# The sums of the LSTM weights' quarters: made in every phase, or made once and loaded

## The chip, the cores and the metric

The kernel runs on one core of a Trainium2 chip. The metric is the device time of one execution in microseconds (us); a lower time is better. The chip offers TensorE (PE in the profile; its weight loads are PEld), VectorE (DVE), ScalarE (ACT), GpSimd (POOL) and SyncE (SP), which issues most DMAs. POOL can issue DMAs too.

## The reference, cut to what matters

The model has four layers on x of 128 graphs, 64 nodes and 256 features. Each normalises x, cuts it at zero, runs a graph network and adds the result to x. The change lies in layer 0, which is two graph convolutions followed by four LSTMs with windows of 1, 2, 3 and 4 nodes:

```python
h = relu(einsum('ts,bsh->bth', adj, x @ Wg0 + bg0))
h = relu(einsum('ts,bsh->bth', adj, h @ Wg1 + bg1))
for p in range(1, 5):
    nw = T // p
    wins = h[:, :nw * p, :].reshape(B * nw, p, H)
    last = lstm_last(Wih[p - 1], Whh[p - 1], bih[p - 1], bhh[p - 1], wins)
    h = h.at[:, arange(nw) * p + (p - 1), :].set(last)
```

and in the LSTM, from a zero state, for every step:

```python
g = x_t @ Wih.T + h @ Whh.T + bias
i, f, gg, o = split(g, 4)
c = sigmoid(f) * c + sigmoid(i) * tanh(gg)
h = sigmoid(o) * tanh(c)
```

Each of Wih and Whh is 1024 x 256 in float32 for each window.

## The kernel before

**Stages.** The 8192 tokens are 16 chunks of 512, or 4 groups of 2048. In the profiled execution the convolutions of all chunks take the first 190 us, the LSTM phases follow until about 1255 us, and layers 1 to 3 fill the rest. Half of the groups stay in the on-chip memory for the LSTM (hTs0); the output of the convolutions for the other half waits in DRAM (hmem).

**The convolutions.** `graph_convolutions(n)` is a generator for one chunk: it loads x three chunks ahead (`load_x`, L540, four buffers), normalises (statistics on DVE, L96; scaling on ACT, L120), aggregates, projects and aggregates again. A loop over 20 values of n moves the chunks under way on by one step each; the tables of later layers (`edge_tables`, `late_tables`) are made in small steps between them. One of these is dinv (L247) on POOL.

**The products of an LSTM.** A product of a weight and an operand is not made from its four quarters with eight smaller products, but with seven, from sums of quarters of the weight and sums of blocks of the operand. For each gate q, `product` issues these with the numbers 1 to 7. On the side of the weight the factors are: 1 is a11, 2 is a12, 3 is s4, 4 is a22, 5 is s1, 6 is s2 and 7 is a11 - a21, where s1 = a21 + a22, s2 = s1 - a11 and s4 = a12 - s2. The number 6 follows the pair 1 and 2, then 7, 5, 3 and 4 (`gate`, L780). The operand's sums are `xop`, made in `prepare` (L700): by ACT copies and DVE sums (L724 to L735), or on POOL when the step beside is a first one ("apart"). The sums of a state h are made on DVE (L858 to L862).

**The weights.** `Weights(kind, w)` (L494) loads one weight of 1024 KB from its input (L500) with one DMA on SP and makes the four sums for all gates on POOL (L512). Weights of the kind "ih" have two buffers, those of "hh" one. Windows 1 and 2 get theirs during the convolutions (n == 2, L652). There are eight phases: windows 1 to 4 for the first half of the groups, and again for the second. When a phase ends, `phase_over` orders the "ih" weight two phases on, eight slots later, and makes the "hh" weight of the next phase at once. So each weight of windows 1 to 4 that a phase uses is loaded and summed twice in a run; there is no "hh" for window 1. After the last phase the buffer of an "ih" weight serves as `x_first`, the first input of layer 1 (L1009).

**The order.** Instructions given to `late` keep the order in which the program makes them; the others are placed by a scheduler, which also places DMAs on SP's and POOL's queues. Each queue then runs in order: an instruction that waits holds up those behind it. A pool's tile of the same tag takes the place of an earlier one when that is released.

Of the kernel before, what the change touches and what calls it, by code (L numbers as in the profile page):

```python
# [9 lines left out]
F32 = mybir.dt.float32  # L10
# [4 lines left out]
ALU = mybir.AluOpType  # L15
AX = mybir.AxisListType

P = 128
T = 64
D = 256  # L20
# [3 lines left out]
MAX_SKIP = 4  # L24
# [7 lines left out]
def gnn_stack_kernel(ctx: ExitStack, tc: tile.TileContext, a: dict, out: bass.AP):  # L32
    nc = tc.nc
# [5 lines left out]
    dram = ctx.enter_context(tc.tile_pool(name="dram", bufs=1, space=bass.MemoryType.DRAM))  # L39
# [4 lines left out]
    def bank():  # L44
        return psums["now"].tile([P, 512], F32, tag="bank", name="bank", bufs=psums["banks"])
# [32 lines left out]
    def late(ins):  # L78

        tc.keep_in_program_order(ins)  # L80
# [4 lines left out]
    class Norm:  # L85


        def __init__(self, xt, root_on_scalar=False, keep=late, mv=None):
            self.xt, self.root_on_scalar, self.keep, self.h, self.mv = xt, root_on_scalar, keep, None, mv
            self.known = mv is not None  # L90
            if mv is None:
                self.st = stat.tile([P, 4, 6], F32, tag="ln_st", name="ln_st")
                self.mv = stat.tile([P, 4, 2], F32, tag="ln_mv", name="ln_mv")
# [79 lines left out]
    def transpose_features(h, dst, ip, keep=None):  # L173

        p = bank()
        for i2 in range(2):
            for c in range(2):
                k = (i2 * 2 + c) * P
                ins = nc.tensor.transpose(p[:, k : k + P], h[:, 2 * ip + i2, c * P : (c + 1) * P], ident)
                if keep and k == 0:  # L180
                    keep(ins)
        nc.scalar.activation(
            dst[:, :, ip * 256 : (ip + 1) * 256].rearrange("p c (i t) -> p i c t", i=2),
            p.rearrange("p (i c t) -> p i c t", i=2, c=2),
            AF.Relu,
        )
# [96 lines left out]
    keep = tabs.tile([P, E], F32, tag="keep", name="keep")  # L283
# [201 lines left out]
    with ExitStack() as l0:  # L485
        wsp = l0.enter_context(tc.tile_pool(name="wsp", bufs=1))
# [4 lines left out]

        class Weights:  # L494
            def __init__(self, kind, w, keep=lambda ins: None):
                bufs = 2 if kind == "ih" else 1
                t = wsp.tile([P, 2, 4, 2, P], F32, tag=f"w{kind}", name=f"w{kind}", bufs=bufs)
                s = wsp.tile([P, 3, 4, P], F32, tag=f"s{kind}", name=f"s{kind}", bufs=bufs)
                keep(
                    nc.sync.dma_start(  # L500
                        out=t.rearrange("p k q j m -> p k (q j m)"), in_=a[f"W{kind}T"][:, w - 1]
                    )
                )
                a11, a12, a21, a22 = t[:, 0, :, 0, :], t[:, 1, :, 0, :], t[:, 0, :, 1, :], t[:, 1, :, 1, :]
                s1, s2, s4 = s[:, 0], s[:, 1], s[:, 2]
                for o, x, y, op in (
                    (s1, a21, a22, ALU.add),
                    (s2, s1, a11, ALU.subtract),
                    (s4, a12, s2, ALU.subtract),
                    (a21, a11, a21, ALU.subtract),  # L510
                ):
                    keep(nc.gpsimd.tensor_tensor(o, x, y, op))  # L512
                self.of = {1: a11, 2: a12, 3: s4, 4: a22, 5: s1, 6: s2, 7: a21}

            def __call__(self, k, q):
                return self.of[k][:, q, :]

        bias = w0.tile([P, MAX_SKIP, 8], F32, tag="bias", name="bias")
        bias2 = w0.tile([P, MAX_SKIP, 8], F32, tag="bias2", name="bias2")
# [2 lines left out]
        weights = {}  # L522


        with ExitStack() as conv:
# [4 lines left out]
            def cpool(name, bufs):  # L530
                return conv.enter_context(tc.tile_pool(name=name, bufs=bufs, reuse_waits="tile"))
# [3 lines left out]
            wc = cpool("wc", 1)  # L535
# [34 lines left out]
            p = bank()  # L570
# [66 lines left out]

            tables = chain(edge_tables(), late_tables())
            under_way = []
            for n in range(NCH + 4):  # L640
                if n < NCH:
                    under_way.append(graph_convolutions(n))

                turns = under_way[-1:] + under_way[:-1] if n < NCH else list(under_way)
                if n == 1:
                    turns += under_way[-1:]
                for one in turns:
                    if next(one, 0) == 0:
                        under_way.remove(one)
                    if n >= 3:  # L650
                        next(tables, None)
                if n == 2:  # L652
                    weights["ih", 0], weights["ih", 1] = Weights("ih", 1), Weights("ih", 2)
                    weights["hh", 1] = Weights("hh", 2)
                    late(nc.vector.tensor_tensor(bias, bias, bias2, ALU.add))
            for _ in tables:
                pass
# [207 lines left out]
        steps, phases = [], []  # L865
        for half in range(2):
            ga, gb = 2 * half, 2 * half + 1
            for w in range(1, MAX_SKIP + 1):
                ph = len(phases)
# [82 lines left out]
        for slot in range(len(tasks) + 2):  # L952
            new = tasks[slot] if slot < len(tasks) else None
            if slot == len(tasks):

                for _ in norm_steps:
                    pass
                first_hT = gp.tile([P, 4 * NMAX], F32, tag="gate", name="hT1_first")
                first_hT = first_hT[:, : 2 * CHUNK].rearrange("p (c t) -> p c t", c=2)
                for ip in range(2):  # L960
                    transpose_features(norms1[0].h, first_hT, ip, late)
            if new:
                step = steps[new[0]]
                one = step.gate(new[1])
                next(one)
            if len(flight) > 1:
                old = flight.pop(0)
                next(old[1], None)
                if new:
                    some_out(slot)  # L970
                measure(2)
                next(flight[-1][1])
            elif flight and not new:
                old = flight.pop(0)
                next(old[1], None)
            else:
                old = None
                if flight:
                    next(flight[-1][1])
            if new:  # L980
                next(one)
                flight.append((new, one))
                at, k = new[0], new[2]
                some_out(slot)
            measure(2)
            if new:

                new_half = at + 1 < len(steps) and at and steps[at + 1].w == 1 < step.w
                if k == len(step.gates) - (1 if new_half else 2) and at + 1 < len(steps):
                    steps[at + 1].prepare(step)  # L990
                if step.w == MAX_SKIP and step.t == 2 and k < 2 and step.g < NGR - 1:
                    for u in range(2):
                        n = 4 * step.g + 2 * u + k
                        later.append((slot, "x", n))
            while later and later[0][0] <= slot:
                _, kind, n = later.pop(0)
                residual[n] = fetch_x(n)
            next(norm_steps, None)
            while later_weights and later_weights[0][0] <= slot:
                _, ph = later_weights.pop(0)  # L1000
                weights["ih", ph] = Weights("ih", phases[ph], late)
            if old:
                (at, q, k), step = old[0], steps[old[0][0]]
                if k == len(step.gates) - 1:
                    if at + 1 == len(steps) or steps[at + 1].phase != step.phase:
                        phase_over(step.phase)
                    if step.phase == len(phases) - 1 and step.t == 1 and step.g == NGR - 1:

                        t_ = wsp.tile([P, 2, 4, 2, P], F32, tag="wih", name="x_first", bufs=2)  # L1009
                        flat = t_.rearrange("p k q j m -> p k (q j m)")  # L1010
                        norms1 = {}
                        for n in range(2):
                            xt = flat[:, n, :].rearrange("p (i d) -> p i d", i=4)
                            nc.sync.dma_start(out=xt, in_=xa[n])
                            norms1[n] = Norm(xt)
                        norm_steps = first_norms1(norms1)
                    if step.w == MAX_SKIP and step.t == MAX_SKIP - 1:
                        outs += [(slot + 1, step.g, c, u, ip) for c in range(2) for u in range(2) for ip in range(2)]
# [6 lines left out]
    with ExitStack() as l1:  # L1025
# [32 lines left out]
        for g, c, u, ip in last_outs:  # L1058
            if not ip:
                n = 4 * g + 2 * u + c  # L1060
# [524 lines left out]
    with ExitStack() as l2:  # L1585
# [55 lines left out]
        with ExitStack() as dense2:  # L1641
# [67 lines left out]
            with ExitStack() as first_dense:  # L1709
# [43 lines left out]
                for slot, (pr, m2) in enumerate(tasks):  # L1753
                    n = slot + 3
# [131 lines left out]
        for k in range(2):  # L1886
            f = t4.tile([P, 4, P], F32, tag=f"field{k}", name=f"field{k}", bufs=1)
# [409 lines left out]
```

## Time and profile before

| | |
|---|---|
| median of 3 runs | 1953.12 us (1952.43 to 1953.27) |
| the profiled execution | 1953.8 us, span 1952.0 us |
| TensorE's granted clock | 0.998 |
| PE busy | 1914.7 us, 98% |
| POOL busy | 463.7 us, 24% |
| moved by DMA | 135.57 MB, mean 69 GB/s |

A line of a timeline gives the start in us from the span's start, the duration, the engine, the line of the kernel, the operation, the tile written and the tiles read, the shape and how many were merged; in brackets stands the idle time of the engine just before and what ended it. A matmul of 128x256 in float32 starts 0.22 us after the one before when nothing holds it up; its own duration in the timeline is longer, since matmuls overlap. In the lines of DMA issues the last number is the median time from issue to landing in us. In lines of waits stand who waited, for whom, the total in us, how often and the longest.

### The profile page before, as it was taken

What the parts mean: (1) busy time and instruction counts of PE and PEld (TensorE: products, weight loads), DVE (VectorE), ACT (ScalarE), POOL (GpSimd) and SP (SyncE); (2) the same over time, 40 slices, a digit from 0 to 9 for tenths busy, and PEclk for the clock granted to TensorE, in tenths of its full rate; (3) what the DMA queues carried; (4) which work ended last, traced back from release to release, by engine and by line L of the source; (5) the groups of instructions that cost most, each with busy time, mean ns of one, the idle gap of its engine ahead of it and who ended that gap; (6) DMA issues with size and microseconds to landing.
All of it is one profiled execution on the core that took longest, in us unless ns stands there. A gap on an engine that the chain in (4) does not pass through costs nothing. (4 is left out here: it accounts for less than half of the span.)

```text
span 1952.0 us, 25195 instructions
## 1 busy us (share of the span) xinstructions
PE 1914.7 (98%) x9150; PEld 1394.8 (71%) x9150; DVE 1329.1 (68%) x2506; ACT 1162.7 (60%) x2169; POOL 463.7 (24%) x614
## 2 busy tenths in 40 slices
PE   9999999999999999999999999999999999999998
PEld 7777468866678874788666788876666775544787
DVE  8775675574475567755744755788788777787887
ACT  4353775564565547755644656588786556592554
POOL 3000031140030002310400200166775510000584
PEclk9999999999999999999999999999999999999999
DMA  7513000010010044000100100342334841022112
GB/s 262 186 50 108 0 22 1 1 44 0 1 43 1 1 151 151 22 1 1 44 0 1 44 1 17 125 166 76 114 136 164 291 152 54 1 66 85 44 66 87
DMA packets 63885, 135.57 MB, mean 69 GB/s; under 512 B 6673, under 2 KB 41361, under 8 KB 61457
## 3 DMA queue, kind: packets, MB, share of 16 engines
q1 hardware_dynamic: 59824, 124.33, 18.7%
q0 software_dynamic: 3328, 9.44, 1.3%
q8 instruction: 72, 1.18, 0.2%
q14 instruction: 53, 0.43, 0.1%
q10 hardware_dynamic: 608, 0.20, 0.0%
HBM read 87.55 MB, written 46.40 MB: 69 GB/s over the span
## 5 line engine op out<-in xcount | busy, mean ns | idle before, releaser
L773 ACT ACTIVATE gate<-gate,bias 128x256 f32<-128x256 f32 (+2 forms) x368 | 247.1, 678 | 176.2 <-DVE gate L789 94.2
L745 PE MATMUL pa<-xop,sih 128*128 128x256 f32 (+2 forms) x1056 | 342.4, 417 | 4.9 <-DVE gate L799 4.7
L745 PEld LDWEIGHTS pa<-xop,sih 128*128 128x128 f32 x1056 | 198.4, 190 | 76.1 <-issue 18.9
L745 PE MATMUL pc<-xop,wih 128*128 128x256 f32 (+2 forms) x736 | 251.1, 423 | 0.0
L789 DVE TENSOR_TENSOR gate<-pb,gate 128x256 f32<-128x256 f32 (+2 forms) x184 | 87.5, 476 | 223.6 <-PE pb L745 151.3
L745 PE MATMUL pa<-lstm_h,shh 128*128 128x256 f32 (+1 forms) x672 | 212.7, 398 | 0.0
L745 PEld LDWEIGHTS pc<-xop,wih 128*128 128x128 f32 x736 | 139.8, 190 | 51.2 <-issue 22.5
L806 DVE TENSOR_TENSOR gate<-pc,gate 128x256 f32<-128x256 f32 (+2 forms) x184 | 87.5, 476 | 110.7 <-PE pc L745 110.1
L1149 ACT ACTIVATE lr<-pair 128x1024 f32<-128x1024 f32 x128 | 124.3, 1024 | 44.0 <-ACT xv L1133 16.2
L745 PEld LDWEIGHTS pa<-lstm_h,shh 128*128 128x128 f32 x672 | 127.7, 190 | 30.2
L745 PE MATMUL pc<-lstm_h,whh 128*128 128x256 f32 (+1 forms) x448 | 141.8, 398 | 0.0
L788 ACT COPY gate<-pa 128x256 f32<-128x256 f32 (+2 forms) x184 | 76.0, 413 | 85.6 <-PE pa L745 85.1
L1114 PE MATMUL bank<-wlv,hT 128*128 128x260 f32 x480 | 116.3, 383 | 4.4 <-DVE xq L1125 3.2
L799 DVE TENSOR_TENSOR gate<-pa,gate 128x256 f32<-128x256 f32 (+2 forms) x184 | 87.3, 475 | 41.4 <-PE pa L745 40.6
L773 ACT ACTIVATE gate<-pa,bias 128x256 f32<-128x256 f32 (+2 forms) x184 | 93.9, 510 | 31.1 <-PE pa L745 29.3
L793 ACT COPY gate<-pa 128x256 f32<-128x256 f32 (+2 forms) x184 | 75.3, 409 | 56.2 <-PE pa L745 55.1
L745 PE MATMUL pa<-xop,wih 128*128 128x256 f32 (+1 forms) x320 | 101.6, 399 | 1.4 <-ACT xop L724 1.2
L1114 PEld LDWEIGHTS bank<-wlv,hT 128*128 128x128 f32 x480 | 87.9, 190 | 20.5 <-DVE xq L1125 5.5
L745 PE MATMUL pb<-xop,wih 128*128 128x256 f32 (+1 forms) x320 | 100.6, 398 | 0.0
L745 PEld LDWEIGHTS pc<-lstm_h,whh 128*128 128x128 f32 x448 | 85.1, 190 | 20.1
L512 POOL TENSOR_TENSOR shh<-whh 128x512 f32<-128x512 f32 x6 | 7.6, 1270 | 379.9 <-DMA whh<-in_WhhT 257.1
L796 ACT COPY gate<-pc 128x256 f32<-128x256 f32 (+2 forms) x136 | 57.9, 425 | 53.0 <-PE pc L745 52.4
(380 smaller groups left out, 4024.5 us busy)
## 6 DMA issues: line engine op xcount, KB each, us to landing
field<-keep SPq DMA_DIRECT2D x4, 2304.0 KB, 13.0
wih<-in_WihT SPq DMA_DIRECT2D x8, 1024.0 KB, 7.0
xres<-in_x SPq DMA_DIRECT2D x16, 512.0 KB, 4.5
xa<-xres POOLq DMA_DIRECT2D x16, 512.0 KB, 3.8
xin<-xb SPq DMA_DIRECT2D x16, 512.0 KB, 3.8
h<-xb SPq DMA_DIRECT2D x16, 512.0 KB, 3.6
xin<-in_x SPq DMA_DIRECT2D x15, 512.0 KB, 6.2
out_x<-h SPq DMA_DIRECT2D x15, 512.0 KB, 2.9
```

The lines of the kernel that those rows point to most:

```text
L512: keep(nc.gpsimd.tensor_tensor(o, x, y, op))
L745: ins = nc.tensor.matmul(p[:, : self.N], weights[kind, self.phase](k, q), x[k], start=first_ and kind == "ih", stop=kind == "hh" or not se ...
L773: nc.scalar.activation(out, in_, AF.Tanh if q == 2 else AF.Sigmoid, bias=bias[:, self.w - 1, 2 * q + j : 2 * q + j + 1],)
L788: nc.scalar.copy(blk[0, 0], pa[:, :N])
L789: nc.vector.tensor_tensor(blk[0, 0], pb[:, :N], blk[0, 0], ALU.add)
L793: nc.scalar.copy(blk[1, 0], pa[:, :N])
L796: (nc.vector.tensor_copy if not self.t and self.w > 1 else nc.scalar.copy)(blk[1, 1], pc[:, :N])
L799: nc.vector.tensor_tensor(blk[1, 1], pa[:, :N], blk[1, 1], ALU.add)
L806: nc.vector.tensor_tensor(blk[1, 0], pc[:, :N], blk[1, 0], ALU.add)
L1114: ins = nc.tensor.matmul(o, hTs[n][:, k, i * P : (i + 1) * P], wlv[:, k, cols], start=k == 0, stop=k == 1)
L1149: nc.scalar.activation(lr, p, AF.Relu)
```

## The change

During the convolutions, the first use of a weight fills one tile of seven parts in the order of the products, [128, 7, 4, 128] (1792 KB): four DMAs bring a11, a12, a21 and a22 to the parts 0, 1, 6 and 3, and POOL makes the sums in place. POOL then stores the tile in DRAM (`quarters0`). The weights of windows 1 and 2 stay where they are for their first phase. The weights of windows 3 and 4 are made in halves of two gates, in eight rounds, in a tile `ahead` with one buffer, one round for each n from 4 on. Every later use is one load of 1792 KB from `quarters0` and has no sums.

```diff
+        quarters0 = {
+            (kind, w): dram.tile([P, 7, 4, P], F32, tag=f"q{kind}{w}", name=f"q{kind}{w}")
+            for kind in ("ih", "hh")
+            for w in range(1, MAX_SKIP + 1)
+        }
+
+        def quarter_weights(v, kind, w, q):
+
+            given = a[f"W{kind}T"][:, w - 1].rearrange("p k (q j m) -> p k q j m", q=4, j=2)
+            for at, k, j in ((0, 0, 0), (1, 1, 0), (6, 0, 1), (3, 1, 1)):
+                nc.sync.dma_start(out=v[:, at], in_=given[:, k, q, j, :])
+            a11, a12, s4, a22, s1, s2, a21 = (v[:, at] for at in range(7))
+            for o, x, y, op in (
+                (s1, a21, a22, ALU.add),
+                (s2, s1, a11, ALU.subtract),
+                (s4, a12, s2, ALU.subtract),
+                (a21, a11, a21, ALU.subtract),
+            ):
+                nc.gpsimd.tensor_tensor(o, x, y, op)
+            nc.gpsimd.dma_start(out=quarters0[kind, w][:, :, q, :], in_=v)
+
         class Weights:
-            def __init__(self, kind, w, keep=lambda ins: None):
-                bufs = 2 if kind == "ih" else 1
-                t = wsp.tile([P, 2, 4, 2, P], F32, tag=f"w{kind}", name=f"w{kind}", bufs=bufs)
-                s = wsp.tile([P, 3, 4, P], F32, tag=f"s{kind}", name=f"s{kind}", bufs=bufs)
-                keep(
-                    nc.sync.dma_start(
-                        out=t.rearrange("p k q j m -> p k (q j m)"), in_=a[f"W{kind}T"][:, w - 1]
-                    )
+            def __init__(self, kind, w, first_time=False, keep=lambda ins: None):
+                self.v = wsp.tile(
+                    [P, 7, 4, P], F32, tag=f"w{kind}", name=f"w{kind}", bufs=2 if kind == "ih" else 1
                 )
-                a11, a12, a21, a22 = t[:, 0, :, 0, :], t[:, 1, :, 0, :], t[:, 0, :, 1, :], t[:, 1, :, 1, :]
-                s1, s2, s4 = s[:, 0], s[:, 1], s[:, 2]
-                for o, x, y, op in (
...
-                    keep(nc.gpsimd.tensor_tensor(o, x, y, op))
-                self.of = {1: a11, 2: a12, 3: s4, 4: a22, 5: s1, 6: s2, 7: a21}
+                if first_time:
+                    quarter_weights(self.v, kind, w, slice(0, 4))
+                else:
+                    keep(nc.sync.dma_start(out=self.v, in_=quarters0[kind, w]))
 
             def __call__(self, k, q):
-                return self.of[k][:, q, :]
+                return self.v[:, k - 1, q, :]
...
+            ahead = [(kind, w, q) for w in (3, 4) for kind in ("ih", "hh") for q in (0, 2)]
             for n in range(NCH + 4):
...
+                if n > 3 and ahead:
+                    kind, w, q = ahead.pop(0)
+                    v = wc.tile([P, 7, 2, P], F32, tag="ahead", name="ahead")
+                    quarter_weights(v, kind, w, slice(q, q + 2))
                 if n == 2:
-                    weights["ih", 0], weights["ih", 1] = Weights("ih", 1), Weights("ih", 2)
-                    weights["hh", 1] = Weights("hh", 2)
+                    weights["ih", 0], weights["ih", 1] = Weights("ih", 1, True), Weights("ih", 2, True)
+                    weights["hh", 1] = Weights("hh", 2, True)
...
-                weights["ih", ph] = Weights("ih", phases[ph], late)
+                weights["ih", ph] = Weights("ih", phases[ph], keep=late)
...
-                        t_ = wsp.tile([P, 2, 4, 2, P], F32, tag="wih", name="x_first", bufs=2)
-                        flat = t_.rearrange("p k q j m -> p k (q j m)")
+                        t_ = wsp.tile([P, 7, 4, P], F32, tag="wih", name="x_first", bufs=2)
+                        flat = t_.rearrange("p s q m -> p (s q m)")[:, : 8 * D].rearrange("p (n x) -> p n x", n=2)
```

The on-chip memory for the weights stays the same in all (wih and sih, whh and shh were 8192 and 6144 bytes of a partition); `ahead` takes 7168 bytes of a partition during the convolutions. The products, their order and their operands are the same.

More of the change, by code (lines that the diff above doesn't have):

```diff
@@ L489, in gnn_stack_kernel @@
         hmem = {n: dram.tile([P, 2, CHUNK], F32, tag=f"hm{n}", name=f"hm{n}") for n in range(NCH // 2, NCH)}
-        class Weights:
-            def __init__(self, kind, w, keep=lambda ins: None):
-                bufs = 2 if kind == "ih" else 1
-                t = wsp.tile([P, 2, 4, 2, P], F32, tag=f"w{kind}", name=f"w{kind}", bufs=bufs)
-                s = wsp.tile([P, 3, 4, P], F32, tag=f"s{kind}", name=f"s{kind}", bufs=bufs)
-                keep(
-                    nc.sync.dma_start(
-                        out=t.rearrange("p k q j m -> p k (q j m)"), in_=a[f"W{kind}T"][:, w - 1]
-                    )
-                )
-                a11, a12, a21, a22 = t[:, 0, :, 0, :], t[:, 1, :, 0, :], t[:, 0, :, 1, :], t[:, 1, :, 1, :]
-                s1, s2, s4 = s[:, 0], s[:, 1], s[:, 2]
-                for o, x, y, op in (
[L507 to L512, printed above, removed]
-                self.of = {1: a11, 2: a12, 3: s4, 4: a22, 5: s1, 6: s2, 7: a21}
```

## The prediction

> **What bounds the kernel now.** I read the page first, then the busy time by stretches, then PE, POOL, DVE and DMA through the stretches where the weight sums run.
>
> ```profile
> PE 1914.7 (98%) x9150; PEld 1394.8 (71%) x9150; DVE 1329.1 (68%) x2506; ACT 1162.7 (60%) x2169; POOL 463.7 (24%) x614
> ...
> DMA  7513000010010044000100100342334841022112
> ```
>
> PE is busy for 98% of the span, so a change that leaves the matmuls alone can only move PE's few pauses. DMA digits (48.8 us each) are high in the first two: the convolutions start with much traffic and end with little.
>
> ```profile
> 0.00:190.00 190.00, 185.81 (x953) 140.70 (x953) 131.27 (x361) 78.47 (x148) 17.66 (x26) 1.00 0.45 153
> 262.00:405.00 143.00, 142.44 (x644) 121.84 (x643) 89.00 (x156) 88.37 (x184) 28.73 (x32) 1.00 0.05 15
> 405.00:555.00 150.00, 149.47 (x535) 101.10 (x534) 83.63 (x121) 80.38 (x143) 19.73 (x15) 1.00 0.04 13
> 555.00:712.00 157.00, 154.71 (x722) 134.60 (x721) 88.94 (x151) 85.92 (x178) 20.15 (x17) 1.00 0.06 22
> 40.00:60.00 20.00, 19.96 (x105) 15.36 (x106) 19.39 (x57) 9.25 (x19) 0.00 (x0) 1.00 1.06 356
> 80.00:100.00 20.00, 19.79 (x106) 14.52 (x105) 16.20 (x40) 6.78 (x13) 0.00 (x0) 1.00 0.09 27
> ```
>
> The columns are PE, PEld, DVE, ACT and POOL busy, PE's granted clock, DMA share and GB/s. In the convolutions (first row) PE pauses 4.2 us of 190; in the LSTM phases with windows of 2, 3 and 4 it pauses 0.6, 0.5 and 2.3 us. The clock is full. The gain is to come from the LSTM rows, and any loss from the first.
>
> **What the sums cost now.** The move out of window 3 into window 4:
>
> ```profile
> 556.77 1.27 POOL L512 TENSOR_TENSOR shh<-whh 128x512 f32<-128x512 f32 x1 [128.25 <-DMA whh<-in_WhhT]
> 558.12 1.33 POOL L512 TENSOR_TENSOR shh<-shh,whh 128x512 f32<-128x512 f32 x1
> ...
> 562.56 1.78 POOL L724 COPY xop<-hT 128x256 f32<-128x256 f32 x2 [0.46 <-ACT gate L773]
> ```
>
> Four sums take 5.3 us here. The operand copies (L724) behind them wait another 0.46 us for ACT, so POOL's order does not delay them. What the sums do is slow DVE. The same DVE instruction in the first half (under a sum) and in the second half (its sums start 0.36 us later, at 1090.40):
>
> ```profile
> 557.08 1.24 DVE L734 TENSOR_TENSOR xop<-xop 128x256 f32<-128x256 f32 x1
> ...
> 1090.04 0.42 DVE L734 TENSOR_TENSOR xop<-xop 128x256 f32<-128x256 f32 x1
> ```
>
> and PE at the same two places:
>
> ```profile
> 557.09 1.03 PE L745 MATMUL pb<-xop,wih 128*128 128x256 f32 x4
> 558.71 0.70 PE L745 MATMUL pa<-xop,sih 128*128 128x256 f32 x2 [0.60 <-DVE gate L799]
> ...
> 1090.04 1.03 PE L745 MATMUL pb<-xop,wih 128*128 128x256 f32 x4
> 1090.90 0.65 PE L745 MATMUL pa<-xop,sih 128*128 128x256 f32 x2
> ```
>
> From the four pb products to the next pa product is 1.62 us in the first half and 0.86 in the second: the sums cost PE 0.76 us there, and the trace holds its own control.
>
> **The change part by part.** *LSTM, removed:* 11 of the 14 sets of sums, 11 x (1.27 + 1.33 + 1.27 + 1.28) = 57 us of POOL. POOL is not the bound; what counts is three sorts of place.
> (a) 558.71: 0.76 us and 0.05 of a slower restart (0.70 against 0.65): 0.8. Bounds 0 to 0.8; the control says 0.8.
> (b) Window 2 into 3, at 408.24 and 941.22. L735 takes 1.24 us under a sum and 0.50 without, and PE then idles 0.46 us on DVE's L799, which ends at 408.18. 0.74 us sooner it would end at 407.44, but ACT's copy out of the same pa (L788) ends only at 407.96, so PE gains 0.2 to 0.3. Bounds 0 to 0.7 each; I take 0.25 twice, since ACT is the next in line: 0.5.
> (c) 569.95 and 1101.61, idle 1.06 and 0.49 us, also on DVE's L799. Here the slow DVE steps (L858 at 1.80 against 1.22 us) run under POOL's operand work, which stays. In the second half that work does queue behind the sums (1096.50 at once after them, ACT's L773 done at 1094.68), so it will start up to 1.8 us sooner, and may then look like the first half, 0.57 us worse. Bounds -0.6 to +1.55; I take 0.
> Sum of the LSTM gain: 0.8 + 0.5 + 0 = 1.3 us, ends -0.6 and +3.8.
>
> The SBUF page of the Trainium skill (State Buffer, section "two separate sides") says DVE instructions with two SBUF inputs and GpSimd exclude each other for a whole instruction. The trace agrees in size: 0.42 became 1.24, which is less than one sum of 1.27 more.
>
> *LSTM, changed:* 11 loads of 1792 KB in place of 1024.
>
> ```profile
> wih<-in_WihT SPq DMA_DIRECT2D x8, 1024.0 KB, 7.0
> ...
> xin<-in_x SPq DMA_DIRECT2D x15, 512.0 KB, 6.2
> ...
> whh<-in_WhhT SPq DMA_DIRECT2D x6, 1024.0 KB, 5.3
> dense<-field SPq DMA_DIRECT2D x3, 2048.0 KB, 8.0
> ```
>
> Between whh (1024 KB, 5.3 us) and dense (2048 KB, 8.0) a 1792 KB load is 7.3 us, against 5.3 + 5.2 until the last sum now. Hidden weights issued at 551.68 are first used at 567.86, so they land 9 us ahead of need; if that cover went, each load would cost at most 7.3 us. Behind whh at 724.55 in SP's queue stand an x and an h load (727.40, 732.57) that land some 2 us later; DVE uses such loads with little to spare in places (it waited 0.74 us at 725.99). Bounds 0 to 2 us, counted 0 since PE is not idle there on a load.
>
> *Convolutions, added:* SP issues 44 weight loads where it had 3: 41 x 0.33 to 0.50 = 14 to 20 us of SP. POOL gets 32 half-wide sums; its row for 128x256 is 0.73 us, so 23 us, and 11 stores, 0.53 to 0.79 us for 512 KB, at most 3.5 times that: up to 30 us. POOL was busy 17.7 of 190. DMA moves 12.8 MB of stores and 4.2 MB of loads more: 17 MB at the 356 GB/s of the full stretch is 48 us on top of 0.45 x 190 = 85, so 133 of 190. The new weight loads read runs of 512 bytes where an x load reads 1 KB; no row has such runs, so their 7.3 MB take between 20 us (the same rate) and 41 us (half of it), and the total 133 to 154. All fit if they only lie beside; the x loads are what must not be late. The one issued at 71.65 has its statistics at 111.67, that of 104.45 at 133.64: with 3.8 us to land (the quiet case) 36 and 25 us to spare. I count 0. Below nothing: PE's 0.75 us idle at 40.04 (on ACT's h1T) could go if the edge tables' DVE work moves.
>
> Sum: profiled 1953.8 (span 1952.0 and 1.8 around it) - 1.3 = 1952.5; the median of the three runs lies 0.7 under the profiled one, so **1951.8**. Case range: 1949.3 to 1953.7 (ends of the LSTM terms). 0.2% of this kernel is 3.9 us, about what a measurement can tell from no change.
>
> **Rivals.**
> *Slower: one buffer for the halves made ahead.* The tile `ahead` has one buffer, so SP's loads of a half wait until POOL's store of the one before has landed, and whatever stands behind them on SP waits too: x loads, stores of h.
>
> ```profile
> SPq L540 <- DVE ln_st L96: 33.7, 5, 17.0
> ...
> POOL dinv L247 <- DVE dinv L246: 101.3, 1, 101.3
> ```
>
> SP already sits in order on x buffers (17 us the longest), and dinv on POOL (134.78) is needed by DVE at 136.48. A round in quiet: 1.5 to issue, 3.8 to land, 2.9 of sums, 0.6 of issue, 3.8 to land = 12.6 us; a convolution takes 190/16 = 11.9. While DMA is full (40 to 72 us) x loads took 13.5 to 14.2 us, so a round is 20 us longer. Two such rounds and 0.7 on each of eight give a lag of 46 us where x loads had 25 to 36 spare: 10 to 20 us lost, if SP's order puts the x loads behind. It decides once the lag passes 25 us; then about +12, 1964. Against it: the order is laid out by a scheduler that has kept PE at 98% here, and may put x loads ahead. The same SBUF page warns that a DMA issued by GpSimd waits for its descriptors while DVE holds the shared port: 3.1 us against 0.62. By that each round would be 2.5 us longer and the lag 20 us more. The trace shows less: POOL's xa stores land in 3.8 us, SP's hm stores of the same size in 2.8.
> *Faster by more:* all upper ends, 3.8 + 0.75 = 4.5 us: 1948.6. It needs ACT not to be next in (b), and (c) to come from the sums.
> *No effect:* something next in line everywhere, 1953.1.
>
> **How the numbers follow.** Forecast 0.30, no effect 0.12: together "same" 0.42. One buffer 0.38, over 0.2% slower. All upper ends 0.20, over 0.2% faster. 1947.5 to 1966 leaves out some 0.05 below and 0.13 above.
>
> **What would show it.** Right: 558.71's wait gone; DVE's L734 and L735 at 0.42 to 0.50 in every phase change; weights landing in 7 to 8 us; PE still at 185 to 186 us of its first 190. Wrong: DVE waiting on an x load or dinv in the convolutions, the LSTM starting later than 190 us, or the wait at 569.95 gone too.

## The result and the profile after

The changed kernel takes 1973.42 us (median of 4 runs, 1972.05 to 1973.93) against 1953.19 us in the runs of the kernel before beside it (1952.43 to 1954.19): a ratio of 1.0102, 95% interval 1.009 to 1.0113. It is 20.2 us slower. The profiled execution took 1972.05 us, with a span of 1970.3. In the kernel after, lines up to 490 keep their numbers and those of the LSTM stand 15 lower down the file (L745 is now L760, L799 is L814).

The page's busy row and its rows of PE's clock and of DMA, to be read against the lines shown in the prediction:

```profile
PE 1916.3 (97%) x9150; PEld 1397.3 (71%) x9150; DVE 1321.8 (67%) x2506; ACT 1162.4 (59%) x2169; POOL 429.5 (22%) x613
...
PEclk9998999999999999999999999999999999999999
DMA  9944010010010026100100100342333941012112
```

POOL does less in all (429.5 us against 463.7), and the DMA digits of the third and fourth slice have risen from 1 and 3 to 4 and 4. PE's granted clock has a dip in the fourth slice (148 to 197 us). The busy time by stretches, with the columns as before; the LSTM's stretches are set 19.5 us later:

```profile
0.00:190.00 190.00, 168.82 (x843) 126.42 (x844) 122.70 (x349) 73.54 (x140) 49.66 (x69) 0.96 0.73 235
30.00:40.00 10.00, 5.52 (x13) 2.85 (x11) 5.34 (x26) 1.91 (x5) 8.41 (x8) 0.66 0.74 258
160.00:166.00 6.00, 4.10 (x16) 3.83 (x17) 4.17 (x13) 4.97 (x11) 0.47 (x1) 0.50 0.45 156
424.50:574.50 150.00, 149.77 (x537) 101.43 (x536) 83.47 (x121) 80.73 (x141) 8.12 (x7) 1.00 0.06 25
574.50:731.50 157.00, 155.34 (x728) 135.93 (x727) 88.40 (x153) 87.00 (x182) 8.14 (x9) 1.00 0.10 36
```

The loss lies in the first row: PE is busy for 168.8 of the first 190 us, where it was for 185.8, and it runs at a lower clock in two places (0.66 and 0.50). The two LSTM rows are better than before by 0.3 and 0.6 us. The LSTM's first product starts at 212.20 us instead of 190.90: 21.3 us were lost in the convolutions. By 1247 us of the kernel before the distance has shrunk to 18.85, so the LSTM gained 2.45 us.

**The first loss, 7.8 us by the product ident,wide (96.55 against 88.79).** The chain of timeline lines, each with the wait in front of it:

```profile
34.38 0.72 DVE L345 TENSOR_SCALAR diag_a<-ident,acol 128x128 f32<-128x128 f32 x2 [7.66 <-DMA acol<-in_a]
35.05 1.20 PE L350 MATMUL bank<-diag_a,ones 128*128 128x128 f32 x4 [4.48 <-DVE diag_a L345]
36.04 5.41 PE L51 MATMUL bank<-aggT,wg 128*128 128x512 f32 x8
```

and the same DVE step in the kernel before:

```profile
28.66 1.26 DVE L345 TENSOR_SCALAR diag_a<-ident,acol 128x128 f32<-128x128 f32 x2 [1.10 <-DMA acol<-in_a]
```

DVE waits 7.66 us for acol, a load of 1 KB, where it waited 1.1. SP issued it 25.5 us into the span (22.3 before), behind the twelve loads that bring the quarters of the first three weights. It took 8.8 us to land (6.4 before), while POOL's store of the first weight was under way. PE idles 4.48 us for DVE, and then runs at half speed until 39.7 us: a product of 128x512 starts every 0.85 us, against 0.43 from 40.0 on. Half of some 4.8 us is 2.4. With 0.8 more on h1T at 47.26 (1.56 us idle, 0.75 before) the sum is 7.7. Two smaller terms nearly cancel: at 27 us the changed kernel had been 0.8 us ahead, and small delays up to 96.55 take 0.9.

**The second loss, 13.5 us.** POOL, DVE and PE around 160 us:

```profile
158.95 0.90 POOL L513 DMA_DIRECT2D qhh<-ahead  x1 [0.30 <-POOL ahead L512]
159.73 0.74 POOL L247 TENSOR_TENSOR dinv<-dinv,half_power 128x1 f32<-128x1 f32 x1
160.51 0.23 DVE L250 COPY dinv_b<-dinv 128x128 f32<-128x128 f32 x1 [16.20 <-POOL dinv L247]
161.16 0.68 DVE L628 TENSOR_TENSOR aggT<-bank,bg 128x512 f32<-128x512 f32 x1
161.90 2.93 PE L51 MATMUL bank<-bdA,aggT 128*128 128x128 f32 x12 [11.32 <-DVE aggT L628]
```

and DVE's copy in the kernel before:

```profile
136.48 0.21 DVE L250 COPY dinv_b<-dinv 128x128 f32<-128x128 f32 x1
```

POOL's power for dinv (L247), one column of 128 values, stands in POOL's queue behind the last of the eight stores of `ahead`. Its input was ready at 142.4. DVE's copy of it (L250) waits 16.2 us at the head of DVE's queue (not at all before), and aggT (L628), which has nothing to do with dinv, stands behind the copy. PE idles 11.32 us and then takes 0.43 us for a product of 128x256 instead of 0.22 until about 166 us: 2.1 us more.

**The LSTM's gain.** The place that the prediction called (a):

```profile
577.73 0.42 DVE L749 TENSOR_TENSOR xop<-xop 128x256 f32<-128x256 f32 x1
...
577.73 1.03 PE L760 MATMUL pb<-xop,wih 128*128 128x256 f32 x4
578.59 0.65 PE L760 MATMUL pa<-xop,wih 128*128 128x256 f32 x2
...
1120.71 0.70 PE L760 MATMUL pa<-xop,wih 128*128 128x256 f32 x2 [1.07 <-DVE gate L814]
```

The DVE sum takes 0.42 us where it took 1.24 under a sum of POOL, and the pa product follows 0.86 us after the pb products, as in the control of the second half. The last line is the second half's place (c): 1.07 us idle instead of 0.49.

### The profile page after: what moved, and what is told of

It is laid out like the page before. It is cut to its first block, busy times and chain, and to the rows that moved or that the text cites. A ratio compares the mean times of both kernels' runs of the same rounds, so it can differ in the third digit from the quotient of the medians.

```text
span 1970.3 us, 25283 instructions
## 1 busy us (share of the span) xinstructions
PE 1916.3 (97%) x9150; PEld 1397.3 (71%) x9150; DVE 1321.8 (67%) x2506; ACT 1162.4 (59%) x2169; POOL 429.5 (22%) x613
## 5 line engine op out<-in xcount | busy, mean ns | idle before, releaser
L760 PE MATMUL pa<-xop,wih 128*128 128x256 f32 (+2 forms) x1376 | 442.5, 412 | 5.5 <-DVE gate L814 4.2
L788 ACT ACTIVATE gate<-gate,bias 128x256 f32<-128x256 f32 (+2 forms) x368 | 247.5, 679 | 174.2 <-DVE gate L804 90.8
L760 PEld LDWEIGHTS pa<-xop,wih 128*128 128x128 f32 x1376 | 259.2, 190 | 90.7 <-issue 19.6
L760 PE MATMUL pa<-lstm_h,whh 128*128 128x256 f32 (+1 forms) x896 | 283.6, 398 | 0.0
L760 PE MATMUL pc<-xop,wih 128*128 128x256 f32 (+2 forms) x736 | 251.2, 423 | 0.0
L760 PEld LDWEIGHTS pa<-lstm_h,whh 128*128 128x128 f32 x896 | 170.4, 190 | 40.1
L760 PEld LDWEIGHTS pc<-xop,wih 128*128 128x128 f32 x736 | 139.9, 190 | 51.1 <-issue 22.5
L739 POOL COPY xop<-hT 128x256 f32<-128x256 f32 (+1 forms) x24 | 11.4, 505 | 702.2 <-ACT gate L788 284.4
L1164 ACT ACTIVATE lr<-pair 128x1024 f32<-128x1024 f32 x128 | 124.2, 1024 | 43.9 <-PE pair L1158 16.9
L760 PE MATMUL pc<-lstm_h,whh 128*128 128x256 f32 (+1 forms) x448 | 141.8, 398 | 0.0
L814 DVE TENSOR_TENSOR gate<-pa,gate 128x256 f32<-128x256 f32 (+2 forms) x184 | 87.4, 475 | 41.5 <-PE pa L760 40.7
L788 ACT ACTIVATE gate<-pa,bias 128x256 f32<-128x256 f32 (+2 forms) x184 | 93.8, 510 | 30.7 <-PE pa L760 28.8
L760 PE MATMUL pb<-xop,wih 128*128 128x256 f32 (+1 forms) x320 | 100.6, 398 | 0.0
L760 PEld LDWEIGHTS pc<-lstm_h,whh 128*128 128x128 f32 x448 | 85.2, 190 | 20.0
L811 ACT COPY gate<-pc 128x256 f32<-128x256 f32 (+2 forms) x136 | 57.8, 425 | 54.4 <-PE pc L760 53.8
L1170 DVE SCALAR_TENSOR_TENSOR lr<-lr,fold 128x1024 f32<-128x1024 f32 x64 | 82.5, 1289 | 3.9 <-ACT lr L1164 1.9
## 6 DMA issues: line engine op xcount, KB each, us to landing
wih<-qih SPq DMA_DIRECT2D x6, 1792.0 KB, 10.1
```

Of the source, the lines that this page charges most:

```text
L760: ins = nc.tensor.matmul(p[:, : self.N], weights[kind, self.phase](k, q), x[k], start=first_ and kind == "ih", stop=kind == "hh" or not se ...
L788: nc.scalar.activation(out, in_, AF.Tanh if q == 2 else AF.Sigmoid, bias=bias[:, self.w - 1, 2 * q + j : 2 * q + j + 1],)
L811: (nc.vector.tensor_copy if not self.t and self.w > 1 else nc.scalar.copy)(blk[1, 1], pc[:, :N])
L814: nc.vector.tensor_tensor(blk[1, 1], pa[:, :N], blk[1, 1], ALU.add)
L1164: nc.scalar.activation(lr, p, AF.Relu)
L1170: late(nc.vector.scalar_tensor_tensor(lrs[1], lrs[0], fold, lrs[1], ALU.mult, ALU.add))
```

## The experiments

Two waits had been found, and one queue behind each. The theory after the result: dinv behind the rounds on POOL costs 13.5 us, acol behind the weights' loads and beside POOL's stores costs 7.7, and the rest of the change gains some 2 us.

| version | median, us | ratio to before | 95% interval |
|---|---|---|---|
| the change | 1973.42 | 1.0102 | 1.0090 to 1.0113 |
| dinv off POOL | 1961.57 | 1.0041 | 1.0029 to 1.0054 |
| acol's loads on ACT's queue | 1974.82 | 1.0103 | 1.0084 to 1.0122 |
| both | 1959.96 | 1.0037 | 1.0023 to 1.0050 |
| no first stores | 1964.02 | 1.0050 | 1.0031 to 1.0069 |
| sixteen rounds, two buffers | 1968.88 | 1.0069 | 1.0047 to 1.0090 |
| acol early, dinv off POOL | 1963.40 | 1.0048 | 1.0030 to 1.0066 |
| the same, no first stores | 1959.70 | 1.0024 | 1.0011 to 1.0036 |
| before, acol early | 1956.76 | 1.0012 | 0.9997 to 1.0027 |
| windows 3 and 4 only, dinv off POOL | 1953.99 | 0.9998 | 0.9988 to 1.0007 |
| before, dinv off POOL | 1953.56 | 0.9996 | 0.9987 to 1.0006 |
| before, hidden sums a slot later | 1953.77 | 1.0002 | 0.9993 to 1.0011 |

The kernel before had a median of 1953.19 us beside the change and of 1953.7 to 1954.1 us beside the other versions.

**dinv off POOL.** The power is made as a square root on ACT and a reciprocal on DVE:

```diff
-            nc.gpsimd.tensor_tensor(dinv, dinv, half_power[:, 0:1], ALU.pow)
+            nc.scalar.activation(dinv, dinv, AF.Sqrt)
+            nc.vector.reciprocal(dinv, dinv)
```

> Edit: the changed kernel, but dinv is made by ACT (a square root) and DVE (a reciprocal) and no longer on POOL. Theory 1 (POOL's queue: dinv stands behind the eighth half made ahead, and DVE's dinv_b waits 16.2 us for it): DVE no longer waits there, PE's idle 11.3 us at 161.90 and the slow clock after it go, some 13.5 us: 1959 to 1961. Rival A (SP's backlog: w3T, issued at 154.21, and the h stores come just as late, and are next in line): PE then waits for one of these at about 158, and only 2 to 6 us come back: 1967 to 1971. Rival B (the convolutions lose to DMA or SBUF traffic in general): no change, 1972 to 1974.

Measured: 1.0041, some 12 us less than the change. There is no wait at 161 us, though POOL's last store is issued at 158.82 as before. The LSTM's first product starts at 198.06. So the rounds themselves may end late; only what stands behind them costs. The first loss stays: `ident,wide` at 95.94, and DVE waits 6.4 us for acol.

**acol's loads on ACT's queue**, and both edits together:

```diff
-            nc.sync.dma_start(out=acol, in_=a["a1"])
+            nc.scalar.dma_start(out=acol, in_=a["a1"])
...
-                    nc.sync.dma_start(
+                    nc.scalar.dma_start(
```

> Edit: the changed kernel, but the nine small loads of acol and ahalf are issued by ACT, not SP, so that they do not stand behind the weights in SP's ring. Theory 1: DVE's wait of 7.7 us for acol at 34.38 goes, PE comes out of the first 50 us some 7 us sooner; but dinv's time (159.73) is set by the eight rounds, not by PE, so the wait before 161.90 grows by most of what was won: 1969 to 1973. Rival C (the two losses are independent and add): 1965 to 1967.

> Edit: both edits, dinv off POOL and acol and ahalf from ACT's queue. Theory 1: both waits go and the LSTM's gain of 2.4 us stays: 1950.5 to 1953. Rival A: w3T or the h stores hold PE at about 158, which costs more now that PE is 7 us ahead: 1960 to 1968. Rival B: over 1965.

Measured: 1.0103 and 1.0037, so moving acol gained nothing by itself and nothing that can be told from noise beside the other edit (the intervals overlap), and the second expectation was wrong. DVE no longer waits for acol in either, and `ident,wide` still starts at 96.08 and 96.52. The nine loads are put early on ACT's queue, and at the start ACT is what the convolutions wait for. In the first version PE idles 3.48 us at 11.07 us, in the second 3.87 at 10.96, both on ACT's h (L120), where the kernel before idles 0.38. The wait at dinv stayed in the first version (PE idles 11.99 us at 162.10). The edit traded one queue for another; it can't tell what the first loss consists of.

**No first stores.** Weights of windows 1 and 2 are not stored when they are made first, and the second half of the groups makes their sums again:

```diff
+            if store:
-            nc.gpsimd.dma_start(out=quarters0[kind, w][:, :, q, :], in_=v)
+                nc.gpsimd.dma_start(out=quarters0[kind, w][:, :, q, :], in_=v)
...
-                if first_time:
-                    quarter_weights(self.v, kind, w, slice(0, 4))
+                if w < 3:
+                    quarter_weights(self.v, kind, w, slice(0, 4), False)
```

> Edit: the changed kernel, but the weights of windows 1 and 2 are not stored; the second half of the groups loads and sums them again. This takes 5.5 MB of stores out of 24 to 48 us. If the stores hold up acol in the DMA engines, it lands at about 30 in place of 34.4 and DVE waits 3 to 4 us in place of 7.7; the rounds start some 8 us sooner and dinv follows at about 150, so PE wins 3 to 4 and 6 to 9 us: 1960 to 1964. If the short runs of 512 bytes are what holds acol, it lands at about 33 and PE wins 1 us there: 1963 to 1967 with the rounds, and 1972 without.

Measured: 1.0050, at the upper end of the first expectation. The three stores bear on both losses. acol lands 4.7 us after its issue instead of 8.8, DVE's wait for it is 3.6, and `ident,wide` starts at 93.21: 3.3 of the 7.8 us are back. The rounds end sooner, dinv comes at 151.61, and PE's idle time there is

```profile
153.78 2.93 PE L51 MATMUL bank<-bdA,aggT 128*128 128x128 f32 x12 [6.53 <-DVE aggT L629]
```

instead of 11.32. The other 4.4 us of the first loss are not from the stores. SP issues acol as late as in the change (25.6 us), and PE idles 2.09 us on h1T at 42.78 and then runs at half speed.

**Sixteen rounds, two buffers.** The same bytes in rounds of one gate, with two buffers of half the size:

```diff
-            ahead = [(kind, w, q) for w in (3, 4) for kind in ("ih", "hh") for q in (0, 2)]
+            ahead = [(kind, w, q) for w in (3, 4) for kind in ("ih", "hh") for q in range(4)]
...
-                if n > 3 and ahead:
+                for _ in range(2 if n > 3 and ahead else 0):
-                    v = wc.tile([P, 7, 2, P], F32, tag="ahead", name="ahead")
-                    quarter_weights(v, kind, w, slice(q, q + 2))
+                    v = wc.tile([P, 7, 1, P], F32, tag="ahead", name="ahead", bufs=2)
+                    quarter_weights(v, kind, w, slice(q, q + 1))
```

> Edit: the changed kernel, but the weights made ahead come in sixteen rounds of one gate, two for each n, in two buffers of half the size (the same memory). dinv stays on POOL. Theory 1 (the rounds follow one another because there is one buffer, and dinv stands behind the last): two rounds now overlap, a pair takes about 11 us where a round took 12.6 to 13, the last store is issued at 142 to 148 in place of 158.95, and dinv with it: PE's wait before its last convolutions shrinks from 11.3 us to 0 to 5, 1960 to 1967. Rival D (DMA and SP set the pace, not the buffer: SP now issues 64 loads, at 0.45 us each 29 us in place of 14): the last store stays at 155 or later, 1971 to 1976.

Measured: 1.0069, between the two expectations. (The profiled execution took 1976.04 us, the longest of the four; part of that was lost in the LSTM, near 287 and 822 us.) The waits of DVE in the convolutions:

```profile
DVE keep L460 <- DMA field<-keep: 8.3, 1, 8.3
DVE diag_a L345 <- DMA acol<-in_a: 7.6, 1, 7.6
DVE dinv_b L250 <- POOL dinv L247: 6.7, 1, 6.7
```

The wait on dinv falls from 16.2 to 6.7, and PE idles 1.83 us there. The last store is issued at 154.85, only 4 us sooner, so the single buffer sets part of the rounds' pace and no more. The wait of `keep`, which may be overwritten only when the stores that read it (L389) are done, was 5.75 us in the changed kernel and is 8.3 here; it is followed by a pause of PE of 3.18 us at 100.25, where the change had 0.50.

**acol early, dinv off POOL**, without and with the first stores left out. acol and ahalf are loaded on SP right behind the first four loads of x, ahead of all weights (shown without the loop for ahalf, which moves with it):

```diff
         if index == 0:
...
-            nc.sync.dma_start(out=acol, in_=a["a1"])
...
+            nc.sync.dma_start(out=acol, in_=a["a1"])
```

> Edit: dinv on ACT and DVE, and acol's and ahalf's loads put on SP ahead of the weights, after the first four x loads. Theory 1: both waits go without the cost that the ACT queue had at the start, the LSTM keeps its 2.4 us; what is left of the loss are the loads of the edge tables (wide, 1.9 us) and the crowded DMA of the first 50 us: 1952 to 1956. Rival E (the crowd itself delays something at once again: x or wide land late and DVE waits as long as before): 1958 to 1962, like the kernel with dinv moved alone.

> Edit: as the one before, and the weights of windows 1 and 2 are not stored (the second half makes their sums again). Theory 1: the first 50 us have 5.5 MB less to move, the second half's two sets of sums for window 2 lie beside phases where PE waits for nothing on them: the convolutions cost at most 1 us more than before the change and the LSTM gains 2 to 2.4 us: 1950.5 to 1953. Rival E: 1955 or more.

> Edit: the kernel before the change, with acol's and ahalf's loads put ahead of the weights on SP. A control: DVE waited 1.1 us for acol there and PE idled 0.75 us at 40.04. If these are one chain, 0.5 to 1.5 us less than the kernel before: 1951.5 to 1953; if not, the same.

Measured: 1.0048, 1.0024 and, for the same move in the kernel before, 1.0012. All three lie above what theory 1 gave, the first above its rival too; the control's interval includes no change. In the control's profile the wait for acol has only moved: DVE waits 1.86 us for it at 13.51, ahead of the statistics of the next x, PE idles 1.97 us at 16.31, and the LSTM's first product starts at 192.34, 1.4 us later. And in the first of them the first weights, now behind nine more loads, are summed from 25.6 to 43 us (19 to 38 in the changed kernel), and the first round made ahead follows up to 47, where DVE makes the edge tables. DVE's timeline there, and POOL's beside it:

```profile
40.12 3.19 DVE L402 COPY spread<-ecol 128x512 f32<-128x512 f32 x1
...
44.72 2.44 DVE L391 TENSOR_SCALAR wide<-wide,key 128x512 f32<-128x512 f32 x1
```

```profile
39.93 0.58 POOL L506 DMA_DIRECT2D qih<-wih  x1
40.52 2.49 POOL L505 TENSOR_TENSOR whh<-whh 128x512 f32<-128x512 f32 x2
...
44.78 2.09 POOL L505 TENSOR_TENSOR ahead<-ahead 128x256 f32<-128x256 f32 x3
```

The other copy of this line takes 0.42 us, the three other steps with a key 0.48. These two end at 43.3 and 47.2, just after POOL's sums beside them (43.0 and 46.9). PE then idles 3.26 us at 44.68 and 2.64 at 48.54 and runs at half speed to 54.4. So to bring acol early does not give the first loss back: the first weights then come late, and DVE is late where it is needed, beside their sums.

**Windows 3 and 4 only, dinv off POOL.** This version was drawn from the runs above: windows 1 and 2 get one load of 1024 KB and their sums in each half, as in the kernel before, and only windows 3 and 4 are made ahead and loaded ready.

```diff
-                if first_time:
-                    quarter_weights(self.v, kind, w, slice(0, 4))
-                else:
+                if w > 2:
                     keep(nc.sync.dma_start(out=self.v, in_=quarters0[kind, w]))
+                    ...
+                    return
+                keep(nc.sync.dma_start(out=flat[:, : 8 * D], in_=a[f"W{kind}T"][:, w - 1].rearrange("p k c -> p (k c)")))
+                ...
+                    keep(nc.gpsimd.tensor_tensor(o, x, y, op))
```

> A version drawn from the runs so far: dinv on ScalarE and VectorE, and of the weights only those of windows 3 and 4 are made ahead and loaded ready; windows 1 and 2 load 1024 KB with one DMA and make their sums in each half as before (no first stores on POOL's queue, no loads of 512-byte runs before the rounds). Theory (the loss lies in the first stores, the short-run loads ahead of acol, and dinv behind the rounds; the gain lies in the hidden weights of windows 3 and 4): the product ident,wide comes back to 88.8 to 90 us, no wait at dinv, the LSTM starts 190.9 to 193 us, its phases gain 2.0 to 2.4 us; ratio 0.9985 to 1.0005. Rival (the rounds themselves, their sums on POOL beside VectorE and their loads, cost the convolutions too): the LSTM starts at 195 us or later, ratio 1.0015 or more.

Measured: 0.9998, 0.9988 to 1.0007. The loss is gone, and the LSTM starts at 191.14. Its busy time by stretches, and PE's two remaining waits in 20 to 190 us:

```profile
0.00:190.00 190.00, 185.56 (x952) 140.53 (x952) 132.32 (x361) 78.67 (x149) 48.91 (x65) 1.00 0.65 213
```

```profile
40.28 3.29 PE L51 MATMUL bank<-wg,h1T 128*128 128x256 f32 x14 [1.74 <-ACT h1T L628]
89.03 0.63 PE L424 MATMUL bank<-ident,wide 128*128 128x128 f32 x4 [0.21 <-DVE wide L420]
```

PE is busy for 185.6 us (185.8 before) although POOL still does 48.9 us of work there and DMA moves 213 GB/s instead of 153. All eight rounds are in this version, so their sums, loads and stores cost the convolutions little: the LSTM starts 1.1 us later than in the kernel before with dinv moved alike (190.05, the first of the two controls below), after the wait of 1.74 us at 40.28 (0.72 there). Against the version with dinv alone moved, it differs only in windows 1 and 2. So the remaining 8 us of that one (1.0041 less 0.9998) come from the way in which their weights are made first, 6.9 of them before the LSTM starts (198.06 against 191.14). Besides the stores that way differs in twelve loads with runs of 512 bytes instead of three, and acol is issued at 20.9 us here instead of 25.5; which of these makes up the 4.4 us that are not from the stores was not separated. In the LSTM its waits at window changes are those of the changed kernel: 568.30 with 1.07 us, 1100.13 with 1.08, none at the place of 558.71. The profile is 1.5 us ahead of the kernel before at 1100.13. The end of the span is not (1952.2 against 1952.0): what was gained is given back in the later layers, 1.2 us of it between 1489 and 1564 us, and the interval can't tell a gain of 2 us from none.

**Two controls on the kernel before.** The first makes dinv on ACT and DVE, with the same three lines as above. The second makes the "hh" weight of the next phase one slot after the end of a phase:

```diff
-                weights["hh", nxt] = Weights("hh", phases[nxt])
+                later_hh.append((slot + 1, nxt))
...
+            while later_hh and later_hh[0][0] <= slot:
+                _, ph = later_hh.pop(0)
+                weights["hh", ph] = Weights("hh", phases[ph], late)
```

> A control: the kernel before with dinv made by ScalarE's square root and VectorE's reciprocal instead of POOL's power, nothing else. Theory (that edit is free, and all that the first experiment gained came from the wait on POOL's queue): within 1 us of the kernel before, ratio 0.9995 to 1.0005. Rival (the edit costs by itself, since ScalarE or VectorE takes it in front of work that is due): ratio 1.001 or more, and 2 us or more of the first experiment's remaining loss belong to it.

> The LSTM's gain without the copy in DRAM: the kernel before with the hidden weight's load and its four sums one slot later than the end of the phase, so that POOL's sums no longer lie under VectorE's operand sums at the phase change. Theory (the gain is the end of the exclusion between POOL's sums and VectorE's two-input instructions, as the second half shows where the sums start 0.36 us later): the PE waits at 408.24, 941.22 and 558.71 go or shrink, the LSTM gains 0.9 to 2.3 us, ratio 0.9988 to 0.9996. Rival (the sums only move onto other VectorE work and hold up the operand copies on POOL behind them): the same or up to 1.5 us slower, with waits at 421 or 569 us longer.

Measured: 0.9996 for dinv, so that edit is free by itself, and the 12 us that it gained in the changed kernel are those of the wait on POOL's queue. The second control, 1.0002, shows nothing on its question: POOL's sums were released by the same product and load as before and ran at the same place (406.13 us before, 405.38 now, with PE 0.75 us ahead there), and the waits at 408, 558 and 941 us stayed. Whether the LSTM's 2 us can be had without the copy in DRAM was not shown.

## Why the prediction was wrong

The forecast was 1951.8 us, the range ended at 1966.0, and the time is 1973.42.

**The step that failed is the one on the convolutions, "I count 0".** They lost 21.3 us. It was worked out from totals: 133 to 154 us of DMA and some 50 more of POOL fit into 190. They did fit: with all eight rounds and without the two waits PE lost 1.1 us at most. What the totals can't show is where the added work stands in a queue. Of the consumers behind it only the x loads were measured against the lag (36 and 25 us to spare). DVE waited for these 0.4 us in all (1.7 before); two small ones were late. Waiting on dinv and a later start of the LSTM had been named as signs of being wrong. The trace of before had shown both, dinv 1.7 us ahead of its use on DVE and acol with 1.1 us of waiting, and neither got a price of its own.

**The "one buffer" rival had the right mechanism, the wrong victim and too small a price.** A quiet round was put at 12.6 us; the stores of the rounds are 11.9 to 13.5 us apart from the third on (96.15 us). In the full stretch they are 25.6 and 15.8 us apart, a delay of some 16 us where 40 were assumed. The last was issued at 158.95. The rival named dinv, but its sum went by x loads and gave 12 us; dinv alone cost 13.5. The first loss was in no rival: a small load that DVE needs early, behind the loads of the first weights and beside their stores.

**A term was missing from every sum: what a pause costs after it.** PE's two long pauses, 4.48 and 11.32 us, were each followed by 4 to 5 us at half speed, which cost 4.5 us in all.

**The LSTM terms.** (a) was right: 0.76 us from pb to pa, as the control said. (b) was mis-sized: both waits went, 0.72 + 0.75 us with their restarts, 1.5 us where 0.5 was taken. The reason given, that ACT's copy (L788) was next in line, did not hold, as the changed kernel's first place shows:

```profile
428.82 0.45 ACT L803 COPY gate<-pa 128x336 f32<-128x336 f32 x1
...
428.92 0.73 PE L760 MATMUL pa<-xop,wih 128*128 128x336 f32 x2
```

PE starts the next pa product 0.1 us after that copy starts, so it had waited for DVE's read alone. (c) came out as its lower end said: unchanged in the first half, 0.57 us worse in the second. These three make 1.7 us. Small stalls near 565, 1097 and 1103 us that no term had held went too, some 1.2 us, and some 0.6 us were lost in places that no term had held either (near 422, 731 and 955 us of the kernel before). The sum is 2.45 us; that it lies inside its ends of -0.6 and 3.8 is in part luck. The loads of 1792 KB land in 7.1 us (whh), where 7.3 was worked out, and in 10.1 (wih, 7.0 before), and PE waits for none.

**The Trainium skill's rule on a DMA issued by GpSimd** (SBUF — State Buffer, section "two separate sides": its descriptors wait while VectorE holds the shared port) would have made each round 2.5 us longer, by the estimate in the prediction. The quiet rounds stayed nearer to the rows: 0.90 us to issue where 0.6 was assumed, and 4.7 us to land 896 KB (qhh) where 3.8 was taken from stores of 512 KB.

## What to carry to other kernels

Work that fits beside a bound engine by its total is free only if nothing urgent stands behind it. For every added instruction that can wait, list what follows it on its own queue, small ones first, with the time at which each is needed; here one column of 128 values behind a store cost five times what the change gained. Add to a pause of PE of 2 us or more the half-speed stretch that followed most of them here, and move the small step off the queue (here two instructions on other engines) before judging the idea. Freed of both losses and kept to windows 3 and 4, this one measured the same as the kernel before.

## What the hardware showed that had not been expected

PE's granted clock fell to 0.50 at a pause, and PE then worked at half speed for 4.2 us (after 11.32 us idle), 4.8 (after 4.48), and 5.1 (after 6.53, in the version without first stores). The time at 0.50 itself, the pause included, was 10.24, 6.83 and 6.83 us. In the thirteen profiles, leaving out the last microseconds of each, the clock falls 27 times, and each time for 3.41 us or two, three or four times that. The Trainium skill (TensorE: Matmul & The Clock Gate, section "Part 1: The HAM clock gate") says that the clock drops to half after an idle window of about 3.4 us and comes back after about 3.4 us of sustained work, and that this window runs free. The length of the window agrees. The pause needed does not: pauses of 2.03, 2.09 and 2.21 us were enough (versions "acol early, dinv off POOL", "no first stores" and "the same, no first stores"), and the clock then fell up to 1.5 us after PE had started again. One of 2.53 us was not followed by a drop (sixteen rounds, 287 us).

DVE instructions with a single input in the on-chip memory took longer beside POOL's work as well, and by more than one of its instructions in a row: 0.42 us became 3.19 for a copy and 0.48 became 2.44 for a step with a key, both ending 0.3 us after POOL's sums. A step of diag_a (L345) took 0.27 us without sums beside it and up to 1.30 with them (no first stores). The prediction had reckoned only with instructions of two inputs, and with one sum at most.
